# First layer of a two-layer graph network: message weights kept in their own PSUM bank, added rows in PSUM, linear terms at the head of a step

## The chip, the cores and the metric

The kernel runs on one core of a Trainium2 chip. The metric is device microseconds of one execution, taken as the median of several. A core has five engines that run side by side, each with its own list of instructions in program order: PE (TensorE: matmuls and transposes, which write PSUM), DVE (VectorE), ACT (ScalarE), POOL (GpSimd, here used to issue indirect gathers) and SP (SyncE, which issues plain DMAs). They meet through semaphores. PSUM, which PE writes, is handed out in banks; this kernel's pools divide eight of them among its stages' tiles.

## The reference, cut to what matters

There are 6250 nodes with 128 features and 206,250 directed edges, sorted by destination. The first layer is a graph attention with 8 heads of 16 features; the second is an equivariant convolution over the same edges, which the change does not touch.

```python
xl = (x @ W_l + b_l).reshape(-1, H, O)
xr = (x @ W_r + b_r).reshape(-1, H, O)
ee = (edge_attr @ W_e).reshape(-1, H, O)
m = leaky_relu(xl[src] + xr[dst] + ee, 0.2)
logits = einsum('eho,ho->eh', m, att)
lmax = segment_max(logits, dst)
exl = exp(logits - lmax[dst])
denom = segment_sum(exl, dst)
alpha = exl / (denom[dst] + 1e-16)
out = segment_sum(xl[src] * alpha[:, :, None], dst)
# then residual + layer norm, FFN of 512 with gelu, layer norm, outer layer norm, second layer
```

## The kernel before, in words

**Stages.** A prologue and `tables` (up to about 225 us) write two tables of projected nodes to DRAM. `attention` is the first layer's loop over edges (about 225 to 2740 us), with `nodes` (residual, layer norms, FFN of finished nodes) fed into it piece by piece. `convolution` is the second layer (to the end).

**Tiles.** A unit is 768 edges, 6 tiles of 128 edges; there are 269 units, and unit k is taken in by step k. Up to 8 units make a batch, 35 in all; most of them have 8. Each edge has 136 values: 8 heads times 17, of which the first 16 are the features of a head and the 17th (`O`) a linear term, the part of the leaky relu that is linear in its input and that can be had from a matmul.

**One step k**, in the order in which the program issues it; since each engine takes its instructions in this order, it is the order of the work on each engine:

- `load(k+2)` (L366, L400 to L406): six gathers of rows of `xl` by POOL, then SP's DMAs for edge attributes, positions, and rows of `xr`.
- `terms(k+1, 0)` and `terms(k+1, 1)`: the pre-activation z of half a unit each, in a PSUM tile of its own (pool `zp`, 3 banks). Matmuls L420 add the edge term and `xr`. The first half gets the rows of `xl` by a matmul with the identity (L423), and then ACT copies its linear terms to `pr` (L426). The second half gets its rows later, on DVE.
- `sum_up` (L551) between the two halves: matmuls that put the sums of an earlier unit into place, in a tile `nd`.
- for a batch whose last unit was E: `rows` at step E+1 (PE transposes the logits, L462, ACT copies them to `lgt`, L463), `peaks` at E+2 (four scans on DVE, L471 to L477, then PE and ACT for `cr`, L482 to L485), `shifts` and `weights` at E+3. `shifts` ends in `gd` and `sd` (L494 to L499). `weights` makes logits minus peak in a PSUM tile (PE, L506 and L508), takes its exp into SBUF as `ex` (ACT, L511), writes the exp of each unit's eight columns into the 17th column of its `xl` (ACT, eight instructions on L514), and makes the scale `s` (PE L516, ACT L518).
- `sums` (L538): twelve matmuls of the weighted rows with a one-hot matrix, into a tile `ag`; ACT copies them to `sb` (L542, L543), which `sum_up` reads one step later.
- `parts(k)` on DVE: L439 multiplies max(z, 0) of the first half by the attention vector; L436 adds z and the rows of `xl` of the second half into `pr` in SBUF, and L439 does the same there.
- a register load on DVE (L597), `places(k+2)` (L411, one-hot of destinations for a later step), `logits` (L445, a reduction of `pr`), `collect` (L557, adds a unit's sums into the accumulator; this frees `nd`).
- for the units that `when` gives this step: `one_hot` (L372) and `messages` (L528, two multiplications of `xl` by `ex` in place, both operands in SBUF).
- one piece of `nodes`.

**PSUM.** Pool `zp` has 3 banks, `mp` 3, `nodes` 2: eight. All tiles named `m` share the three banks of `mp` in turn: `ag` of the sums, `nd`, the transposes, `c_ps`, the weights' `ex_ps` and `s_ps`. A tile waits until the readers of the last tile in its bank are done.

**The plan.** `when` gives the step of each unit's messages: not before E+4, then one unit a step, and two a step near the end (the last 28 units, `ENDING`). Its sums follow one step later, `sum_up` two, `collect` three. An order written in the program is the order of each engine; no scheduler moves instructions.

Of the kernel before, what the change touches and what calls it, by code (L numbers as in the profile page):

```python
# [8 lines left out]
F32 = mybir.dt.float32  # L9
BF16 = mybir.dt.bfloat16  # L10
I32 = mybir.dt.int32
AF = mybir.ActivationFunctionType
OP = mybir.AluOpType
PSUM = bass.MemoryType.PSUM
DRAM = bass.MemoryType.DRAM

P = 128
# [16 lines left out]
R8 = U * 8  # L34
TU = 6
UE = TU * P
W = 32
H = 8
O = D // H
OW = O + 1  # L40
# [67 lines left out]
class Fast:  # L108
# [269 lines left out]
    def attention(self, acc, xlp, xls):  # L378
# [3 lines left out]
        tc, nc, a, NU = self.tc, self.nc, self.a, self.NU  # L382
        with ExitStack() as st:
            def pool(n, b, **k):
                return st.enter_context(tc.tile_pool(name=n, bufs=b, **k))
            ld, wk, b1, b2 = pool("ld", 3), pool("wk", 2), pool("b1", 1), pool("b2", 2)
            zp, mp = pool("zp", 3, space=PSUM), pool("mp", 3, space=PSUM)
            last = b1.tile([H, 1], F32, name="last0")
            nc.vector.memset(last, -BIG)
            of = {u: (b, u - v) for b, (v, m, _) in enumerate(self.batches) for u in range(v, v + m)}  # L390
            ohs, eas, zs, prs, lgs, ms, sbs, nds = {}, {}, {}, {}, {}, {}, {}, {}
# [21 lines left out]
            def terms(u, half):  # L413
                ea, _, xr = eas[u]
                xl, oht = xls[u], ohs[u]
                z = zs[u, half] = zp.tile([P, 3 * ZW], F32, name="z")
                for lhs, rhs in ((ea, self.w3[:, 2]), (oht, xr)):
                    for t in range(3):
                        e = slice((3 * half + t) * P, (3 * half + t + 1) * P)
                        nc.tensor.matmul(z[:, t * ZW:(t + 1) * ZW], lhs[:, e], rhs,  # L420
                                         start=(t == 0 and lhs is ea), stop=(half == 1 and t == 2 and lhs is oht))
                if half == 0:
                    nc.tensor.matmul(z, self.ident, xl[:, :3, :].rearrange("p t f -> p (t f)"),  # L423
                                     start=False, stop=True)
                    prs[u] = wk.tile([P, TU * H, OW], F32, name="pr")
                    nc.scalar.activation(prs[u][:, :3 * H, O], z.rearrange("p (h o) -> p h o", o=OW)[:, :, O], AF.Copy)  # L426
                else:
                    del eas[u], ohs[u]

            def parts(u):  # L430

                for k in range(2):
                    z = zs.pop((u, k)).rearrange("p (h o) -> p h o", o=OW)
                    p = prs[u][:, 3 * H * k:3 * H * (k + 1)]
                    if k:
                        nc.vector.tensor_add(p.rearrange("p h o -> p (h o)"), z.rearrange("p h o -> p (h o)"),  # L436
                                             xls[u][:, 3:, :].rearrange("p t f -> p (t f)"))
                        z = p
                    nc.vector.scalar_tensor_tensor(p[:, :, :O], z[:, :, :O], 0.0, self.attb, op0=OP.max, op1=OP.mult)  # L439

            def logits(u):
                b, i = of[u]
# [59 lines left out]
            def weights(b):  # L502
                R, gd, sd = ws[b]
                lg = lgs.pop(b)
                ex_ps = mp.tile([P, TU, R], F32, name="m")
                nc.tensor.matmul(ex_ps, self.ident, lg[:, :, :R], start=True, stop=False)  # L506
                for t in range(TU):
                    nc.tensor.matmul(ex_ps[:, t, :], gd[:R, t * P:(t + 1) * P], self.negi[:R, :R],  # L508
                                     start=False, stop=(t == TU - 1))
                ex = b2.tile([P, TU, R8], F32, name="ex")  # L510
                nc.scalar.activation(ex[:, :, :R], ex_ps, AF.Exp)  # L511
                for i in range(R // H):
                    xv = xls[self.batches[b][0] + i].rearrange("p t (h o) -> p t h o", o=OW)
                    nc.scalar.activation(xv[:, :, :, O], ex_ps[:, :, i * H:(i + 1) * H], AF.Exp)  # L514
                s_ps = mp.tile([P, U], F32, name="m")
                nc.tensor.matmul(s_ps, self.e128[:R], sd[:R], start=True, stop=True)  # L516
                s = b2.tile([P, U], F32, name="s", bufs=3)
                nc.scalar.activation(s, s_ps, AF.Copy)  # L518
                ws[b] = ex, s

            def messages(u):

                b, i = of[u]
                xl = xls.pop(u)
                xv = xl.rearrange("p t (h o) -> p t h o", o=OW)[:, :, :, :O]
                for t in range(0, TU, 3):
                    v = xv[:, t:t + 3]
                    nc.vector.tensor_mul(  # L528
                        v, v, ws[b][0][:, t:t + 3, i * H:(i + 1) * H, None].to_broadcast([P, 3, H, O]))
                ms[u] = xl, ohs.pop(u)  # L530

            def sums(u):

                xl, oh = ms.pop(u)
                ag = mp.tile([P, ZW], F32, name="m")
                for t in range(TU):
                    q = t % 4
                    nc.tensor.matmul(ag[q * W:(q + 1) * W], oh[:, t, :], xl[:, t, :],  # L538
                                     start=(t < 4), stop=(t + 4 >= TU))
                sb = sbs[u] = wk.tile([P, 2, D], F32, name="sb")  # L540
                av = ag.rearrange("p (h o) -> p h o", o=OW)
                nc.scalar.activation(sb[:, 0].rearrange("p (h o) -> p h o", o=O), av[:, :, :O], AF.Copy)  # L542
                nc.scalar.activation(sb[:, 1].rearrange("p (h o) -> p h o", o=O),  # L543
                                     av[:, :, O:].to_broadcast([P, H, O]), AF.Copy)

            def sum_up(units):
                nd = mp.tile([P, 2, 2, W], F32, name="m")
                for i, u in enumerate(units):
                    sb = sbs.pop(u)
                    for j in range(2):  # L550
                        nc.tensor.matmul(nd[:, i, j], sb[:, j], self.s4, start=True, stop=True)  # L551
                    nds[u] = nd[:, i]
# [4 lines left out]
                nc.vector.scalar_tensor_tensor(v, v, ws[b][1][:, i:i + 1], nds.pop(u), op0=OP.mult, op1=OP.add)  # L557


            when, ready, k = {}, 0, 0  # L560
            for u in range(NU):
                end = self.batches[of[u][0]][2]
                k = max(k, end + (4 if end < NU - 1 else 3))
                busy = {k - 2, k - 3} & {b[2] for b in self.batches}
                if len(when.get(k, ())) == (2 if k >= NU or k > NU - ENDING and not busy else 1):
                    k += 1
                when.setdefault(k, []).append(u)

            AHEAD = 2
            ends = {end: b for b, (_, _, end) in enumerate(self.batches)}  # L570
# [3 lines left out]
            for half in range(2):  # L574
                terms(0, half)
            for k in range(max(when) + 4):
                now, sums_of, ups_of, got = (when.get(k - i, []) for i in range(4))
                if k + AHEAD < NU:
                    load(k + AHEAD)
                if k == 2:  # L580
                    nodes = Queue(self.nodes(st, acc), self.done, 2)
                if k + 1 < NU:
                    terms(k + 1, 0)
                if ups_of:
                    sum_up(ups_of)
                if k + 1 < NU:
                    terms(k + 1, 1)
                if k - 3 in ends:
                    shifts(ends[k - 3])
                    weights(ends[k - 3])  # L590
                if k - 2 in ends:
                    peaks(ends[k - 2])
                for u in sums_of:
                    sums(u)
                if k < NU:
                    parts(k)
                cs = [nc.vector.value_load(self.r0[0:1, u:u + 1], min_val=0, max_val=self.n) for u in got]  # L597
                if k + AHEAD < NU:
                    places(k + AHEAD)
                if k < NU:  # L600
                    logits(k)
                for u, c in zip(got, cs):
                    collect(u, c)
                for u in now:
                    ohs[u] = self.one_hot(wk, u)
                    messages(u)
                if k - 1 in ends:
                    rows(ends[k - 1])
                for _ in range(1 + (k > NU + 3) if k > 1 else 0):
                    nodes.step(max(got, default=-1))  # L610
# [1026 lines left out]
```

## Time and profile before

| what | value |
| --- | --- |
| median of 6 runs | 5966.35 us (5944.16 to 5976.72) |
| the profiled execution's own time | 5954.48 us |
| its span (first to last instruction) | 5952.6 us, so 1.88 us lie around it |
| mean granted TensorE clock | 0.721 of full speed |
| busy: PE, DVE, ACT, POOL | 3948.0 (66%), 2639.9 (44%), 956.0 (16%), 3212.4 (54%) |
| 2780 to 5950 us (second layer): PE, DVE, ACT, POOL busy | 2116.29, 1070.67, 369.12, 1543.84 of 3170 us |
| gathers of the first layer, L366 into `xl` | 1590, mean 1035 ns |
| gathers of the second layer, L366 into `f` | 1614, mean 943 ns |

How to read it: durations of groups are means of one instruction in ns; "idle before" is the time in which the engine had nothing to run just before the group's instructions, and the name behind the arrow is what ended that wait, inferred from semaphore events. "remote" is a release that the records ascribe to no engine of this core, and "issue" a stretch in which the engine waited for nothing that the profile shows. Ends of matmuls are modelled. In a window of the timeline each row is start, duration, engine, line and operation, with the wait ahead of it in brackets.

### The profile page before, as it was taken

To read this page: it belongs to the slowest core of one execution; us is meant where nothing else is said; L and a number is where in the kernel's file an instruction comes from. 1 tells how busy PE (TensorE), PEld (TensorE's weight loads), DVE (VectorE), ACT (ScalarE), POOL (GpSimd) and SP (SyncE) were. 2 spreads that over 40 slices of the span, in tenths; PEclk is the share of its full clock that TensorE was granted. 3 is DMA by queue.
4 is the path that set the end of the run, shared out by engine and by line. 5 is a ranking of instruction groups with operands and counts; after the bars stand their busy time and mean duration, and the time that the engine had idled before them with its cause. 6 is when DMAs were issued, how large, how long until landed. Compare 5 with 4: busy or idle time off the path is not lost.

```text
span 5952.6 us, 67647 instructions
## 1 busy us (share of the span) xinstructions
PE 3948.0 (66%) x21381; PEld 3123.8 (52%) x21381; DVE 2639.9 (44%) x6828; ACT 956.0 (16%) x2528; POOL 3212.4 (54%) x3236
## 2 busy tenths in 40 slices
PE   3666676766666667666666667666666666666666
PEld 2454555555455555445555555555555555555555
DVE  1565556556555556546333333333333333333333
ACT  1111222222222222113111111111111111111111
POOL 6256666666666666652454444544545445454454
PEclk6677777777777777767677776777777767777777
DMA  4444444444434444331111111111111111111111
GB/s 120 128 120 106 105 109 112 114 111 115 113 102 112 108 114 117 102 94 51 39 42 36 41 41 38 42 37 39 42 38 38 40 40 41 39 41 37 39 42 35
DMA packets 290621, 428.25 MB, mean 72 GB/s; under 512 B 122700, under 2 KB 199454, under 8 KB 290254
## 3 DMA queue, kind: packets, MB, share of 16 engines
q0 software_dynamic: 103296, 218.27, 15.5%
q1 hardware_dynamic: 183258, 197.74, 11.3%
q10 hardware_dynamic: 3700, 7.82, 0.4%
q8 instruction: 173, 2.83, 0.2%
q14 instruction: 194, 1.59, 0.1%
HBM read 403.55 MB, written 19.96 MB: 71 GB/s over the span
## 4 chain that ended last, share of the span: by engine, by line
PE 29%; another core or an unknown queue 23%; ACT 4%; issue 2%; DVE 2%; DVEq 0%; DMA 0%; POOL 0%; ACTq 0%
PE y L850 8%; PE h_ps L803 8%; PE w L810 6%; PE y L848 5%; ACT h L804 2%; PE z L420 1%; PE m L538 0%; DVE xl L528 0%; ACT L623 0%; ACT L804 0%; DVE pr L439 0%; PE z L423 0%; ACT v L632 0%; PE n L702 0%
## 5 line engine op out<-in xcount | busy, mean ns | idle before, releaser
L366 POOL DMA_INDIRECT f<-fFEAT,fsrc x1614 | 1522.6, 943 | 1604.5 <-PE y L850 1135.3
L366 POOL DMA_INDIRECT xl<-fXL,fsrc x1590 | 1645.5, 1035 | 999.4 <-issue 425.8
L822 DVE SCALAR_TENSOR_TENSOR os<-at,fl,e 128x128 f32<-128x128 f32 x1614 | 454.4, 344 | 1819.4 <-remote 1013.7
L803 PE MATMUL h_ps<-e,m 128*128 128x384 f32 (+1 forms) x540 | 407.3, 856 | 858.7 <-ACT h L804 853.8
L850 PE MATMUL y<-os,f 128*128 128x96 f32 x3228 | 892.6, 367 | 0.1
L848 PEld LDWEIGHTS y<-os,f 128*128 128x128 f32 x3228 | 704.3, 254 | 190.9 <-issue 80.9
L420 PE MATMUL z<-fw,ea 128*128 128x136 f32 x3228 | 659.4, 350 | 140.4 <-issue 61.2
L804 ACT ACTIVATE h<-h_ps 128x384 f32<-128x384 f32 x540 | 264.6, 490 | 2742.0 <-remote 1280.3
L803 PEld LDWEIGHTS h_ps<-e,m 128*128 128x128 f32 (+1 forms) x540 | 157.2, 322 | 980.6 <-ACT h L804 951.2
L420 PEld LDWEIGHTS z<-fw,ea 128*128 128x128 f32 x3228 | 558.7, 243 | 212.5 <-issue 111.2
L848 PE MATMUL y<-os,f 128*128 128x32 f32 x3228 | 654.7, 290 | 1.6 <-DVE f L831 1.6
L850 PEld LDWEIGHTS y<-os,f 128*128 128x128 f32 x3228 | 649.5, 249 | 0.2 <-DVE f L831 0.2
L810 PE MATMUL w<-wq,h 128*128 128x256 f32 x1620 | 562.7, 482 | 0.0
L538 PE MATMUL m<-xl,oh 128*32 128x136 f32 x3228 | 260.5, 351 | 261.9 <-ACT s L518 92.7
L831 DVE TENSOR_TENSOR f<-w,f 128x384 f32<-128x384 f32 (+1 forms) x810 | 408.7, 546 | 0.0
L810 PEld LDWEIGHTS w<-wq,h 128*128 128x128 f32 x1620 | 356.8, 244 | 41.0 <-issue 0.6
L551 PEld LDWEIGHTS m<-fcst,sb 128*128 128x128 f32 x1076 | 192.4, 236 | 346.6 <-issue 146.6
L803 PE MATMUL h_ps<-h,m 128*128 128x384 f32 x540 | 248.8, 545 | 169.4 <-ACT h L804 145.6
L551 PE MATMUL m<-fcst,sb 128*128 128x32 f32 x1076 | 182.7, 301 | 207.8 <-ACT sb L543 106.1
L423 PE MATMUL z<-xl,fcst 128*128 128x408 f32 x538 | 312.3, 668 | 8.2 <-issue 8.1
L538 PEld LDWEIGHTS m<-xl,oh 128*32 128x32 f32 x3228 | 131.4, 127 | 323.4 <-issue 117.4
L528 DVE TENSOR_TENSOR xl<-xl,ex 128x384 f32<-128x384 f32 x538 | 274.0, 549 | 8.1 <-ACT ex L511 8.1
(145 smaller groups left out, 4093.5 us busy)
## 6 DMA issues: line engine op xcount, KB each, us to landing
ea<-fast_eat_dram SPq DMA_DIRECT2D x269, 384.0 KB
lb<-fLB SPq DMA_DIRECT2D x269, 144.0 KB
f<-fFEAT,fsrc POOLq DMA_INDIRECT x1614
xl<-fXL,fsrc POOLq DMA_INDIRECT x1590
xr<-fXR SPq DMA_DIRECT2D x807, 8.5 KB
e<-fast_e8t_dram SPq DMA_DIRECT2D x16, 384.0 KB
fXR<-pt SPq DMA_DIRECT2D x16, 306.0 KB
fXL<-tb SPq DMA_DIRECT2D x16, 204.0 KB
```

The source lines that it names most:

```text
L366: self.nc.gpsimd.indirect_dma_start(out=to, out_offset=None, in_=table, in_offset=bass.IndirectOffsetOnAxis(ap=self.src[:, g:g + 1], axis=0))
L420: nc.tensor.matmul(z[:, t * ZW:(t + 1) * ZW], lhs[:, e], rhs, start=(t == 0 and lhs is ea), stop=(half == 1 and t == 2 and lhs is oht))
L423: nc.tensor.matmul(z, self.ident, xl[:, :3, :].rearrange("p t f -> p (t f)"), start=False, stop=True)
L538: nc.tensor.matmul(ag[q * W:(q + 1) * W], oh[:, t, :], xl[:, t, :], start=(t < 4), stop=(t + 4 >= TU))
L551: nc.tensor.matmul(nd[:, i, j], sb[:, j], self.s4, start=True, stop=True)
L803: nc.tensor.matmul(ps, m, x[:, s], start=True, stop=True)
L804: nc.scalar.activation((h1s, hs)[k][p][:, s], ps, AF.Gelu_apprx_tanh, scale=sc)
L810: nc.tensor.matmul(w[:, 2 * t:2 * t + 2, :], hs[p][:, e:e + P], wq, start=True, stop=True)
L822: nc.vector.scalar_tensor_tensor(os[:, 2 * t + i], at4, self.l[:, 2 * p + i, c * CT + t:c * CT + t + 1], e4s[p][:, 2 * (c * CT + t) + i, : ...
L831: nc.vector.tensor_mul(vy[:, :, j, 32:].rearrange("p t (c x) -> p t c x", c=3), w[:, :, None, 64 + j * 32:96 + j * 32].to_broadcast([P, n, ...
L848: nc.tensor.matmul(ys[p][:, i, 0], vy[:, e, 0], os[:, e, 3], start=(c == t == i == 0), stop=False)
L850: nc.tensor.matmul(ys[p][:, i, 1:], vy[:, e, 1], os[:, e, :3], start=False, stop=last)
```

## The change

Three things are edited, all of them in `attention`:

1. **Linear terms and additions at the head of a step.** A new function `linear(k)` is the first of step k. On DVE it adds the rows of `xl` to z of the second half, in PSUM and in place (L435 of the new kernel), and on ACT it copies the linear terms of both halves to `pr` (L436, twice a step). Before, only the first half's were copied, one step earlier, right behind L423, and the second half's came out of the addition. `parts` is left with two multiplications (L443), both from PSUM. The register load moves ahead of `parts`.
2. **Message weights in a PSUM bank of their own.** A new pool `xp` with one bank holds `ex`; `mp` goes from 3 banks to 2. The exp is taken in place in PSUM (L515), the eight columns are copied from it (L518, Copy in place of Exp), and the messages (L532) read their factor from PSUM.
3. **The place of `weights`.** Before, it always stood behind `shifts` in step E+3, ahead of the sums. Now a dictionary `due` says where: ahead of the sums as before for 8 of the 35 batches (the first four and the last four), and for the other 27 at the end of step E+3, behind that step's messages (the last ones of the batch before) and ahead of `rows` and of the piece of `nodes`. The steps that `when` gives to the messages are the same in both kernels.

```diff
@@ -384,7 +384,7 @@
             def pool(n, b, **k):
                 return st.enter_context(tc.tile_pool(name=n, bufs=b, **k))
             ld, wk, b1, b2 = pool("ld", 3), pool("wk", 2), pool("b1", 1), pool("b2", 2)
-            zp, mp = pool("zp", 3, space=PSUM), pool("mp", 3, space=PSUM)
+            zp, mp, xp = pool("zp", 3, space=PSUM), pool("mp", 2, space=PSUM), pool("xp", 1, space=PSUM)
             last = b1.tile([H, 1], F32, name="last0")
             nc.vector.memset(last, -BIG)
             of = {u: (b, u - v) for b, (v, m, _) in enumerate(self.batches) for u in range(v, v + m)}
@@ -422,21 +422,26 @@
                 if half == 0:
                     nc.tensor.matmul(z, self.ident, xl[:, :3, :].rearrange("p t f -> p (t f)"),
                                      start=False, stop=True)
-                    prs[u] = wk.tile([P, TU * H, OW], F32, name="pr")
-                    nc.scalar.activation(prs[u][:, :3 * H, O], z.rearrange("p (h o) -> p h o", o=OW)[:, :, O], AF.Copy)
                 else:
                     del eas[u], ohs[u]
 
+            def linear(u):
+
+
+                prs[u] = wk.tile([P, TU * H, OW], F32, name="pr")
+                for k in range(2):
+                    z = zs[u, k]
+                    if k:
+                        nc.vector.tensor_add(z, z, xls[u][:, 3:, :].rearrange("p t f -> p (t f)"))
+                    nc.scalar.activation(prs[u][:, 3 * H * k:3 * H * (k + 1), O],
+                                         z.rearrange("p (h o) -> p h o", o=OW)[:, :, O], AF.Copy)
+
             def parts(u):
 
                 for k in range(2):
                     z = zs.pop((u, k)).rearrange("p (h o) -> p h o", o=OW)
-                    p = prs[u][:, 3 * H * k:3 * H * (k + 1)]
-                    if k:
-                        nc.vector.tensor_add(p.rearrange("p h o -> p (h o)"), z.rearrange("p h o -> p (h o)"),
-                                             xls[u][:, 3:, :].rearrange("p t f -> p (t f)"))
-                        z = p
-                    nc.vector.scalar_tensor_tensor(p[:, :, :O], z[:, :, :O], 0.0, self.attb, op0=OP.max, op1=OP.mult)
+                    nc.vector.scalar_tensor_tensor(prs[u][:, 3 * H * k:3 * H * (k + 1), :O], z[:, :, :O], 0.0,
+                                                   self.attb, op0=OP.max, op1=OP.mult)
 
             def logits(u):
                 b, i = of[u]
@@ -502,16 +507,15 @@
             def weights(b):
                 R, gd, sd = ws[b]
                 lg = lgs.pop(b)
-                ex_ps = mp.tile([P, TU, R], F32, name="m")
-                nc.tensor.matmul(ex_ps, self.ident, lg[:, :, :R], start=True, stop=False)
+                ex = xp.tile([P, TU, R], F32, name="ex")
+                nc.tensor.matmul(ex, self.ident, lg[:, :, :R], start=True, stop=False)
                 for t in range(TU):
-                    nc.tensor.matmul(ex_ps[:, t, :], gd[:R, t * P:(t + 1) * P], self.negi[:R, :R],
+                    nc.tensor.matmul(ex[:, t, :], gd[:R, t * P:(t + 1) * P], self.negi[:R, :R],
                                      start=False, stop=(t == TU - 1))
-                ex = b2.tile([P, TU, R8], F32, name="ex")
-                nc.scalar.activation(ex[:, :, :R], ex_ps, AF.Exp)
+                nc.scalar.activation(ex, ex, AF.Exp)
                 for i in range(R // H):
                     xv = xls[self.batches[b][0] + i].rearrange("p t (h o) -> p t h o", o=OW)
-                    nc.scalar.activation(xv[:, :, :, O], ex_ps[:, :, i * H:(i + 1) * H], AF.Exp)
+                    nc.scalar.activation(xv[:, :, :, O], ex[:, :, i * H:(i + 1) * H], AF.Copy)
                 s_ps = mp.tile([P, U], F32, name="m")
                 nc.tensor.matmul(s_ps, self.e128[:R], sd[:R], start=True, stop=True)
                 s = b2.tile([P, U], F32, name="s", bufs=3)
@@ -557,10 +561,14 @@
                 nc.vector.scalar_tensor_tensor(v, v, ws[b][1][:, i:i + 1], nds.pop(u), op0=OP.mult, op1=OP.add)
 
 
-            when, ready, k = {}, 0, 0
+
+            when, due, k = {}, {}, 0
             for u in range(NU):
-                end = self.batches[of[u][0]][2]
-                k = max(k, end + (4 if end < NU - 1 else 3))
+                b, i = of[u]
+                end = self.batches[b][2]
+                if i == 0:
+                    due[max(k, end + 3), k < end + 3] = b
+                    k = max(k + 1, end + (4 if end < NU - 1 else 3))
                 busy = {k - 2, k - 3} & {b[2] for b in self.batches}
                 if len(when.get(k, ())) == (2 if k >= NU or k > NU - ENDING and not busy else 1):
                     k += 1
@@ -575,6 +583,8 @@
                 terms(0, half)
             for k in range(max(when) + 4):
                 now, sums_of, ups_of, got = (when.get(k - i, []) for i in range(4))
+                if k < NU:
+                    linear(k)
                 if k + AHEAD < NU:
                     load(k + AHEAD)
                 if k == 2:
@@ -587,14 +597,15 @@
                     terms(k + 1, 1)
                 if k - 3 in ends:
                     shifts(ends[k - 3])
-                    weights(ends[k - 3])
+                if (k, True) in due:
+                    weights(due[k, True])
                 if k - 2 in ends:
                     peaks(ends[k - 2])
                 for u in sums_of:
                     sums(u)
+                cs = [nc.vector.value_load(self.r0[0:1, u:u + 1], min_val=0, max_val=self.n) for u in got]
                 if k < NU:
                     parts(k)
-                cs = [nc.vector.value_load(self.r0[0:1, u:u + 1], min_val=0, max_val=self.n) for u in got]
                 if k + AHEAD < NU:
                     places(k + AHEAD)
                 if k < NU:
@@ -604,6 +615,8 @@
                 for u in now:
                     ohs[u] = self.one_hot(wk, u)
                     messages(u)
+                if (k, False) in due:
+                    weights(due[k, False])
                 if k - 1 in ends:
                     rows(ends[k - 1])
                 for _ in range(1 + (k > NU + 3) if k > 1 else 0):
```

## The prediction

> **What bounds the kernel now.** The change touches only the first layer's loop, from about 225 to 2740 us: 269 steps of one unit (768 edges), 9.3 us each. I read first the windows, then the groups by form, the waits of 300 to 2700 us, and the timeline of single steps.
>
> ```profile
> core 0: us, PE busy (x) PEld busy (x) DVE busy (x) ACT busy (x) POOL busy (x), PEclk, DMA share, GB/s
> 1000.00:1500.00 500.00, 354.00 (x2311) 269.16 (x2310) 302.54 (x688) 112.27 (x362) 335.85 (x320) 0.75 0.43 112
> ```
>
> In 500 us no engine is busy over 354 (PE), DVE 303, ACT 112: nothing is full. The step is a ring of handovers, and the waits say which:
>
> ```profile
> ACT sb L542 <- remote: 414.3, 64, 14.2
> ...
> ACT sb L542 <- PE m L538: 203.0, 106, 6.5
> ...
> DVE pr L439 <- ACT pr L426: 136.2, 47, 10.9
> ...
> PE m L551 <- ACT sb L543: 104.3, 32, 8.6
> ...
> PE m L538 <- ACT s L518: 92.4, 22, 12.3
> ...
> PE z L420 <- DVE pr L439: 40.9, 28, 5.4
> ```
>
> (Waited for: total us, times, longest.) ACT's copies of the sums wait for PE, and PE's next matmul waits for those copies. Part of this is no work at all:
>
> ```profile
> 1056.27 0.66 PE L538 MATMUL m<-xl,oh 128*32 128x136 f32 x12
> ...
> 1062.58 0.94 POOL L366 DMA_INDIRECT xl<-fXL,fsrc  x1 [0.30 <-issue]
> ...
> 1065.51 0.28 ACT L542 ACTIVATE sb<-m 128x128 f32<-128x128 f32 x1 [7.16 <-remote]
> ```
>
> The sums ended at 1056.93; the copy that needs only them began 8.6 us later, while seven gathers ran back to back (1056.34 to 1063.5). I call this the **hold**: over 234 steps the timeline gives a mean of 2.99 us from the end of L538 to the start of L542, about half of them under 0.3.
>
> Step lengths from sums to sums, averaged over the full batches by phase p (steps since the batch's last unit), with the hold in brackets: p0 7.15 (4.78), p1 9.39 (3.34), p2 15.27 (0.73; the scans), p3 12.91 (0.21; shifts and weights), p4 6.39 (3.21), p5 6.32 (3.01), p6 7.18 (6.05), p7 11.41 (2.61). In p3 the sums start 6.59 us after the last term matmul, and the timeline shows why:
>
> ```profile
> 1083.01 0.49 ACT L511 ACTIVATE ex<-m 128x384 f32<-128x384 f32 x1 [3.49 <-remote]
> 1083.39 0.35 ACT L514 ACTIVATE xl<-m 128x48 f32<-128x48 f32 x2
> ...
> 1083.99 1.45 ACT L514 ACTIVATE xl<-m 128x48 f32<-128x48 f32 x6 [0.25 <-DMA xl<-fXL,fsrc]
> ...
> 1085.30 0.17 ACT L518 ACTIVATE s<-m 128x8 f32<-128x8 f32 x1
> 1085.49 0.64 PEld L538 LDWEIGHTS m<-xl,oh 128*32 128x32 f32 x12 [4.17 <-ACT s L518]
> ```
>
> Weights, exp, eight copies and s stand ahead of the sums, which take the bank that they held.
>
> **The change, part by part.** Durations are means of 300 to 2700 us:
>
> ```profile
> L528 DVE TENSOR_TENSOR xl<-xl,ex 128x384 f32<-128x384 f32 x496 | 252.6, 549 | 1.9 <-ACT ex L511 1.9
> L436 DVE TENSOR_TENSOR pr<-z,xl 128x408 f32<-128x408 f32 x250 | 143.6, 574 | 171.8 <-remote 65.6 <-PE z L420 47.6 <-PE z L423 30.0
> L439 DVE SCALAR_TENSOR_TENSOR pr<-pr,fattb 128x384 f32<-128x384 f32 x250 | 140.1, 560 | 8.6
> L439 DVE SCALAR_TENSOR_TENSOR pr<-z,fattb 128x384 f32<-128x384 f32 x251 | 136.9, 545 | 210.9 <-ACT pr L426 136.2 <-issue 74.6
> ```
>
> *Durations: no term.* The addition (0.574) moves ahead of the linear copies and now writes PSUM; no row does that, so I bound it by 0.545 (L439 from PSUM) and 0.99 (the reduction L445, the longest of a step) and take 0.574, the same operation. The second L439 reads PSUM instead of SBUF: 0.545 for 0.560. L528 with one factor in PSUM: between 0.545 and 0.574, now 0.549. The exp in place: 0.49 into SBUF, bounds 0.37 and 0.59 (L463 of both sizes). Eight Exp become eight Copy, 0.253 each, nearest the same. The new second linear copy costs 0.211 of ACT a step (L426); it stands on the path and is in the ring below.
>
> The register load moves from behind the additions and products to ahead of them, on DVE. DVE idles 44.2 us before L411, 0.18 a step, which is the most that it can cost today; ahead of the first L439 it lies beside the wait for ACT's copies: nothing, and 0.18 a step (45 us) if DVE is never early there. No DMA moves: the loads keep their place on SP's and POOL's queues, behind nothing new.
>
> *1. Weights out from ahead of the sums.* 27 of the 35 batches place them at the end of step E+3 (E: the batch's last unit); 8 keep the old place. 27 x 6.59 = **-178 us**.
>
> *2. What is late next.* At the end of E+3 the weights wait for the messages of that step (the one bank of ex), and the linear copies of E+4 are queued behind them on ACT. ACT first does sb(E+3): sums 1.06, hold about 3, copies 0.45, nodes' operations 0.8 (some 200 us in 250 steps, 72 of it table loads of 1.283): 5.3 us after the sums began. Then exp 0.49, eight copies 1.77, s 0.17, linear copies 0.3, and the DVE chain from the first L439 to collect (3.2 now, less the addition and some: 2.5): 10.5, and with PE's weights (0.86 + 1.55 + 0.34) partly ahead of the exp up to 12.8. Before p4 took 6.39: +4.1 to +6.4, I take 5.9: 27 x 5.9 = **+159**. Peaks in p2 now wait for collect and two more copies: 0.8 x 31 = **+25**. Cover that would bring both to nothing: PE's terms of the next unit (3 to 4 us in the timeline), which it can do while ACT is held up; in the ring below they lie beside it already.
>
> *3. The ring of ordinary steps.* With two banks in place of three, the sums of a step wait for that step's collect; collect follows the linear copies, which now stand on ACT behind the last step's sb and nodes' work instead of ahead of it. Ring: sums 1.0, hold H, sb 0.45, nodes 0.8, linear copies 0.3, DVE 2.5, handovers 0.25: 5.3 + H. Against the phases above with H as it is: p0 +2.9, p1 0, p5 +2.0, p6 +4.1, p7 0: 9.0 a batch. Yet holds shrink in longer steps (0.73 and 0.21 in p2 and p3); at half of H: +0.5, +0.5, +1.1 = 2.2. I take 4.8, a little nearer to 2.2: 31 x 4.8 = **+149** (bounds 0 and +280). For no cost speaks that collect ends 2.5 us ahead of the sums on average today, and after their start in only 36 of 220 steps.
>
> *4. Ending.* In the last 28 steps, two units a step, 14 sums wait for a sb copy in place of a free bank: 14 x 2.2 = **+30** (0 to +60).
>
> *5. Less disturbance.* Gathers take 1035 ns here and 943 in the second layer; of 319 gathers over 1.05 us, 104 lie beside an L528 and 72 beside an L439. L528 and the second L439 lose an SBUF operand. POOL itself waits for buffers (314 us behind L543), so only bursts and holds shorten: 7% of 3.0 us in 250 steps, 53 us; and PE gives 10.9 signals a step in place of 12.0 (counted in the two instruction lists), 8% of the holds in some 170 ordinary steps, 40 us: **-93** (bounds -150 and 0).
>
> The Trainium skill (SBUF — State Buffer, Who interferes with whom) says that a VectorE instruction with two SBUF inputs contends with GpSimd instructions that read SBUF, and one with at most one doesn't. The 1035 against 943 ns agree with it; by the rule alone 92 ns x 1590 = 146 us of GpSimd time would go, which I don't put on the path.
>
> **Sum:** -178 + 159 + 25 + 149 + 30 - 93 = +92. The profiled execution took 5954.5 us (span 5952.6 and 1.9 around it), 12 under the median: 5954.5 + 92 = 6046, **6045 us**.
>
> **Rivals.** *Faster:* the weights' new place is hidden: PE's terms and DVE's addition cover the chain in E+4. For: PE waits 92 us for s in 22 places, and after the change none of the sums does. Against: the linear copies are behind it on an in-order engine. With term 2's 159 gone: 92 - 159 = -67, **5887**. It decides if E+4 gives back less than 5.9 - 92/27 = 2.5 us. *No change:* holds take up the slack, term 3 is 2.2 a batch: 92 - 81 = +11, **5965**. *Much slower:* holds stay as they are, term 3 is 9.0: 92 + 130 = +222, **6176**.
>
> **The numbers.** Forecast (5975 to 6140, its own range) 0.42; faster 0.34; no change 0.11; much slower 0.13. A measurement tells about 0.3% (18 us) from no change. So faster 0.34, same 0.11, slower 0.55. The range 5850 to 6180 leaves out the ends of both outer cases, about 0.18.
>
> **What would show it.** Right: the sums (now L542) wait for collect (L561) and no longer for s; the linear copies (L436) run right behind the sb copies (L547) or node work; the first L443 waiting on L436 for more than 136 us in all; p3 down by 6 and p4 up by 4 to 6; gathers near 990 ns. Wrong: p4 about 6.4 (then faster), ordinary steps unchanged with holds shorter (no change), or an L435 or L532 much over 0.6 us, which would add their excess to every step, as DVE is in the ring.

## The result: 0.5% slower, and the profile after

The changed kernel takes 5995.67 us (median of 21 runs, 5974.85 to 6006.81) where the kernel before takes 5966.14 (42 runs): a ratio of 1.0045, 95% interval 1.0036 to 1.0054. The forecast was slower, 6045 us; the sign held, the size did not: +29.5 us in place of +79. (The sum itself was +92, set on the profiled execution, which was 12 us under the median.) Kernels that are compared ran on the same chip, but the experiments fell on several chips; on chip 13 both kernels take over a quarter less time and the change is a gain of 3.1%. That turned out to be the key to the first result.

The profiled execution of the changed kernel has a span of 5981.3 us (before 5952.6). Step lengths, from sums to sums, averaged over the full batches as in the prediction (worked out from the trace's rows):

| phase | p0 | p1 | p2 | p3 | p4 | p5 | p6 | p7 | batch |
| --- | --- | --- | --- | --- | --- | --- | --- | --- | --- |
| before | 7.15 | 9.39 | 15.27 | 12.91 | 6.39 | 6.32 | 7.18 | 11.41 | 76.0 |
| after | 9.79 | 9.36 | 14.63 | 6.39 | 12.22 | 6.45 | 8.69 | 8.58 | 76.1 |

The parts move by up to 6.5 us, and the batch stays. From step 24 to 236 the two traces differ by 2.5 us in 2000. Behind step 236 the changed kernel loses 28 us: 14.7 up to step 267, 13.1 from there to the second layer. Only the 13.1 is safe: the three other traces with three `mp` banks (the kernel before again, and twice with late weights) show 96 to 98 us for that drain, like the first (96.5), and all with two banks on this kind of chip 104 to 112. In the stretch up to 267 two traces of the kernel before itself, from different chips, differ by 23.6 us.

The waits of the changed kernel, 300 to 2700 us (total us, times, longest):

```profile
ACT sb L546 <- remote: 685.3, 81, 14.7
DVE pr L443 <- ACT pr L436: 447.2, 133, 13.3
...
ACT sb L546 <- PE m L542: 248.6, 84, 11.4
...
PE z L420 <- DVE pr L443: 75.5, 58, 5.6
...
PEld m L542 <- DVE acc L561: 30.0, 47, 4.7
```

Nothing waits for s ahead of the sums any more (92.4 us before). In its place DVE waits 447 us for the linear copies (136 before), the sums wait in 47 places for collect, and the copies of the sums wait longer for a release that the records ascribe to no engine (685 us for 414). The durations were costed rightly; by form (out and in, partitions by elements), in the same stretch:

```profile
L443 DVE SCALAR_TENSOR_TENSOR pr<-z,fattb 128x384 f32<-128x384 f32 x498 | 253.5, 550 | 587.9 <-ACT pr L436 447.2 <-issue 54.6 <-ACT h L645 23.7
L532 DVE TENSOR_TENSOR xl<-xl,ex 128x384 f32<-128x384 f32 x497 | 250.3, 543 | 0.0
L435 DVE TENSOR_TENSOR z<-z,xl 128x408 f32<-128x408 f32 x249 | 146.2, 587 | 240.1 <-remote 134.3 <-PE z L420 35.9 <-PE m L542 14.7
L515 ACT ACTIVATE ex<-ex 128x384 f32<-128x384 f32 x30 | 14.7, 488 | 44.1 <-PE z L423 12.8 <-remote 10.9 <-PE ex L513 10.2
```

The addition into PSUM takes 587 ns against 574 into SBUF, the multiplication of the messages 543 against 549, exp in place 488 against 490. The gathers, from the page, became faster as the prediction said (972 ns, before 1035):

```profile
L366 POOL DMA_INDIRECT xl<-fXL,fsrc x1590 | 1545.2, 972 | 1111.0 <-issue 414.1
```

### The profile page after: what moved, and what is told of

The parts are those of the page before. It is cut to its first block, busy times and chain, and to the rows that moved or that the text cites. A ratio compares the mean times of both kernels' runs of the same rounds, so it can differ in the third digit from the quotient of the medians.

```text
span 5981.3 us, 67651 instructions
## 1 busy us (share of the span) xinstructions
PE 4007.9 (67%) x21381; PEld 3168.0 (53%) x21381; DVE 2604.8 (44%) x6828; ACT 969.4 (16%) x2797; POOL 3116.1 (52%) x3236
## 4 chain that ended last, share of the span: by engine, by line
PE 30%; another core or an unknown queue 25%; ACT 4%; issue 2%; DVE 2%; DMA 0%; DVEq 0%; ACTq 0%; POOL 0%
PE y L863 8%; PE h_ps L816 8%; PE w L823 6%; PE y L861 5%; ACT h L817 2%; PE z L420 1%; PE m L542 1%; DVE xl L532 0%; ACT L636 0%; PE z L423 0%; DVE pr L443 0%; PE n L715 0%; PE n L723 0%; PE n L746 0%
## 5 line engine op out<-in xcount | busy, mean ns | idle before, releaser
L366 POOL DMA_INDIRECT xl<-fXL,fsrc x1590 | 1545.2, 972 | 1111.0 <-issue 414.1
L420 PE MATMUL z<-fw,ea 128*128 128x136 f32 x3228 | 681.8, 360 | 209.0 <-issue 110.4
L420 PEld LDWEIGHTS z<-fw,ea 128*128 128x128 f32 x3228 | 576.9, 252 | 283.1 <-issue 187.0
L443 DVE SCALAR_TENSOR_TENSOR pr<-z,fattb 128x384 f32<-128x384 f32 x538 | 273.7, 550 | 605.2 <-ACT pr L436 463.9
L542 PE MATMUL m<-xl,oh 128*32 128x136 f32 x3228 | 245.1, 357 | 202.0 <-ACT sb L547 82.9
L423 PE MATMUL z<-xl,fcst 128*128 128x408 f32 x538 | 316.9, 678 | 2.4 <-issue 2.3
L546 ACT ACTIVATE sb<-m 128x128 f32<-128x128 f32 x269 | 74.6, 277 | 1500.4 <-remote 685.3
```

The costliest lines, as they stand in the source:

```text
L366: self.nc.gpsimd.indirect_dma_start(out=to, out_offset=None, in_=table, in_offset=bass.IndirectOffsetOnAxis(ap=self.src[:, g:g + 1], axis=0))
```

## What paces the middle: the hold, seen in both traces

Why does a batch stay at 76 us? The hold of the prediction has a cause that the first trace already shows, in a stage that I had not read. Up to 225 us POOL issues the first units' gathers while PE, ACT and DVE make the second table. Windows of the kernel before (columns as in the prediction):

```profile
125.00:150.00 25.00, 3.38 (x8) 1.90 (x8) 0.58 (x1) 0.51 (x1) 18.90 (x21) 0.50 0.33 89
150.00:175.00 25.00, 3.38 (x8) 1.90 (x8) 1.07 (x2) 0.94 (x2) 15.62 (x17) 0.50 0.30 62
175.00:200.00 25.00, 16.30 (x39) 9.38 (x40) 13.26 (x22) 8.10 (x17) 0.00 (x0) 0.50 0.47 132
```

With 21 gathers in 25 us PE starts 8 matmuls; with none, 39. Its clock is 0.50 in all three rows. The changed kernel on chip 13, in the same stage, with as many gathers:

```profile
75.00:100.00 25.00, 25.00 (x60) 13.99 (x60) 13.12 (x23) 8.38 (x17) 19.21 (x20) 0.50 0.81 193
```

So on the first kind of chip PE and the engines that wait for it hardly get on while gathers run back to back, and on chip 13 they do. I read this as PE's signals (its semaphore updates) being held. That it is the signal and not the matmul that is late is argued, since ends of matmuls are modelled; the starts speak for it. In the changed kernel's trace the twelve matmuls of a unit's sums start within 0.58 us where gathers run and 0.65 us where none do. And of 126 holds over 2 us between steps 24 and 236, PE has started later matmuls more than 1 us before the copy in 109.

Counted from the trace's semaphore events, in the middle of the loop: before, PE gives 0.71 signals in a gather of usual length, 1.33 in a lengthened one, 0.19 in the 0.3 us pause between two, and 5.7 in a longer gap of POOL (2.7 us); on chip 13, 1.36 in a gather and 0.48 in the pause. (The trace of the kernel before holds 5757 of the 6704 updates that PE's instructions should make, that of the changed kernel on chip 13 holds 6302 of 6444, so the counts are only rough.) A hold in the changed kernel's timeline, with the sums and PE's next work:

```profile
1098.70 0.66 PE L542 MATMUL m<-xl,oh 128*32 128x136 f32 x12
...
1100.08 0.94 POOL L366 DMA_INDIRECT xl<-fXL,fsrc  x1 [0.30 <-issue]
...
1100.27 0.90 PE L423 MATMUL z<-xl,fcst 128*128 128x408 f32 x2
...
1102.58 0.95 POOL L366 DMA_INDIRECT xl<-fXL,fsrc  x1 [0.30 <-issue]
...
1104.91 0.28 ACT L546 ACTIVATE sb<-m 128x128 f32<-128x128 f32 x1 [8.58 <-remote]
1105.08 0.27 ACT L547 ACTIVATE sb<-m 128x128 f32<-128x128 f32 x1
...
1105.62 0.95 POOL L366 DMA_INDIRECT xl<-fXL,fsrc  x1 [2.09 <-ACT sb L547]
```

The burst of gathers ends; PE's signal arrives; the sums are copied; that frees an `xl` buffer; the next burst starts. In the changed kernel a burst of six begins within 0.7 us of a sb copy in 82% of the steps, lasts 7.41 us, and 2.11 us pass to the next: 9.52. Before: 7.80 and 1.75, 9.55. The step is a burst and a gap; my reading, which the experiments test, is that what is reordered inside it is paid for, or won back, from the holds.

## The experiments

**The places and the banks, on chip 3.** Four kernels; the kernel before took 6033.9 us there. The times expected below were worked out for the first chip, where it takes 5966, so I compare by the ratio. The changed kernel itself was not run on chip 3. *The kernel before with only the weights moved:*

```diff
-                    weights(ends[k - 3])
+                if (k, True) in due:
+                    weights(due[k, True])
...
+                if (k, False) in due:
+                    weights(due[k, False])
                 if k - 1 in ends:
                     rows(ends[k - 1])
```

> The kernel before, with nothing but the place of the weights changed: for the same 27 batches they stand at the end of step E+3, behind its messages. Theory (the 6.5 us that step p3 loses to the weights are given back in p4 only because the changed kernel queues its linear copies behind them on ACT; before's linear copies of a step are made one step earlier, so they stay ahead): p3 falls from 12.9 to about 6.5 us, p4 stays at 6.4 to 7.5, so 27 x 5.5 = 150 us less: 5800 to 5870 us. Rival (the chain has to be waited for anyway, by the messages of E+4 or by PE through the banks): p4 rises by 5 to 6 us, and the time stays at 5950 to 5985 us.

6029.11 us, ratio 1.0001 (0.9982 to 1.0019): the rival. p3 fell to 6.47 us, and p4 rose to 14.49, with the linear copies not behind the weights at all. PE shows the new wait (300 to 2700 us):

```profile
PE m L551 <- ACT s L518: 62.6, 14, 9.7
```

sum_up of step E+4 stands ahead of the next terms and sums on PE, and waits for s. *The changed kernel with the linear copies ahead of the weights and nodes:*

```diff
-                if k < NU:
-                    linear(k)
...
+                if k + 1 < NU:
+                    linear(k + 1)
                 if (k, False) in due:
                     weights(due[k, False])
```

> The changed kernel, with the additions and linear copies of unit k+1 moved from the head of step k+1 to the end of step k: behind the messages, but ahead of the weights, of rows and of the piece of nodes. Theory (p4 is long because these copies stand behind exp, eight copies and s): p4 falls from 12.2 to 7 or 8 us, 27 x 4.5 = 120 us, and the other steps lose up to 0.8 us of nodes' ACT work each: 5790 to 5880 us. Rival (p4 is long because the messages and sums of E+4 need ex and s themselves, or because of holds): p4 stays above 11 us, and the time at 5975 to 6005 us.

6042.22 us, 1.0011 (1.0000 to 1.0023), p4 12.09 us: the rival for p4; the ratio makes 5973 us of the first chip, just under its times. My reason for a long p4 fell with both. *The changed kernel with the messages' factor in SBUF:*

```diff
-                nc.scalar.activation(ex, ex, AF.Exp)
+                ex_ps, ex = ex, b2.tile([P, TU, R8], F32, name="exs")
+                nc.scalar.activation(ex[:, :, :R], ex_ps, AF.Exp)
```

> The changed kernel, but exp goes to an SBUF tile as before, the eight columns are exp from PSUM as before, and the messages read their factor from SBUF: two SBUF operands again. Theory (gathers are slowed by DVE instructions with two SBUF operands, and longer bursts mean longer holds): mean gather in the first layer up from 972 to 1000 to 1020 ns, and the time up by 15 to 50 us on the changed kernel: 6010 to 6045 us. Rival (POOL runs ahead and its time isn't on the path): gathers slower in the same way, time within 12 us of the changed kernel's, 5984 to 6008 us.

6025.87 us, 0.9990 (0.9975 to 1.0005). The gathers went to 1066 ns, over the theory's 1000 to 1020, so the messages' second SBUF operand is what slows them; the time did not follow. On the first chip's scale it is 5960 us, under the ranges of both. *The changed kernel with one tile for a step's sums:*

```diff
-                ag = mp.tile([P, ZW], F32, name="m")
+                ag = mp.tile([P, 2, ZW], F32, name="m")
```

> The changed kernel, with the sums of a step's units in one PSUM tile (two units share a bank) and one pair of ACT copies for both; nothing changes in steps with one unit. Theory (the whole loss lies in the ending, where 14 sums wait for the first unit's copies because the second unit's tile needs their bank): the stretch from step 236 to the second layer loses its 28 us again, 5962 to 5975 us. Rival (the ending is longer because the linear copies stand behind four sb copies, or because of holds): at most 10 us less, 5985 to 5997 us.

6029.05 us, 1.0000 (0.9987 to 1.0012). By the ratio alone this is the theory's 5966 us. But the two kernels before it have no joint tile and are level too, and the drain behind step 267 took 106.5 us, in place of 109.6 in the first trace: 3 us, not 28. Four kernels with quite different steps (p4 from 11.9 to 14.5 us) lie within 17 us of each other, and a batch takes 76 to 77 us in all of them. That called for a common cause.

**The suspected cause, halved and increased.** The next runs fell on chip 13, where the kernel before takes 4368.61 us. The kernels with fewer or more gathers, or without the edge term, were run once on a chip.

> The changed kernel once more, for comparison with the kernel before and with the other runs on one chip. Theory (the first comparison holds on every chip): 1.0045 times the kernel before, and a batch of eight steps in the middle as long as before's, 76 us. Rival (four variants were level with the kernel before on another chip, so the difference belongs to the chips): 1.000 to 1.002.

4230.35 us, 0.9684 (0.9663 to 0.9705): neither. The holds were gone: 0.09 us a step, against 2.64, and the copies wait for the sums themselves (waits of 150 to 1750 us, trace of the next run of this kernel):

```profile
ACT sb L546 <- PE m L542: 792.5, 208, 9.2
```

*Three of six gathers replaced by a plain DMA:*

```diff
-                    for t in range(TU):
+                    for t in range(TU // 2):
                         self.gather(xls[u][:, t, :], self.XL, u, t)
+                    nc.sync.dma_start(xls[u][:, TU // 2:, :],
+                                      self.XL[:TU // 2 * P].rearrange("(t p) f -> p t f", p=P))
```

> The changed kernel with three of the six gathers of a unit replaced by one plain DMA of other rows of the same table (the rows of half of the edges are thus left out). Theory A (the length of a batch stays at 76 us whatever is reordered because PE's signals get through slowly while gathers run, and the gathers fill 7.4 of 9.5 us): with 3.7 us of gathers a step, the step falls by 2 us or more, 269 x 2 = 540 us, to 5450 us or less. Theory B (the batch is set by a ring of handovers of PE, ACT and DVE that the reorderings only shift): less than 60 us of change. Theory C (DMA traffic): no gain either, or a loss, since as many bytes move.

4011.14 us, 219 less than the changed kernel beside it, and a batch of 52.9 us in place of 60.5. That lies between theory A's 540 and the 60 of B and C. *A seventh gather:*

```diff
+                    self.gather(b2.tile([P, ZW], F32, name="xtra"), self.XL, u, 0)
```

> The changed kernel with a seventh gather per unit, into a tile that nobody reads. Theory A (gathers set the pace): each step longer by most of the 1.25 us from gather to gather, 200 to 330 us in all. Theory B (ring of PE, ACT and DVE; POOL waits 2.1 us a step for buffers): less than 40 us.

4597.02 us, 367 more, over theory A's 200 to 330: 1.36 us for each of 269 units, a little more than the 1.25 from gather to gather. *No matmuls of the edge term:*

```diff
-                for lhs, rhs in ((ea, self.w3[:, 2]), (oht, xr)):
+                for lhs, rhs in ((oht, xr),):
```

> The changed kernel without the six matmuls of the edge term in each unit (edge attributes are left out of the pre-activations; they are still loaded). PE loses 12 of about 37 records a step, some 3.3 us. Theory D (PE at its granted clock sets the pace, its records' ends being only modelled): a step shorter by 2 to 3.3 us, 540 to 880 us in all. Theory A (gathers): less than 100 us. Theory B (ring, in which the terms of the next unit are one link): 100 to 400 us.

4234.26 us, 4 more than the changed kernel: PE's work is not what paces chip 13. Three of these were repeated on the same chip, and the joint sums were run:

> The changed kernel again, beside the next three on one chip. If the copies of the sums start within 0.3 us of the last sum (no holds, as in the run of 4230 us): 0.965 to 0.972 times the kernel before. If there are holds of 2 to 3 us a step: 1.0035 to 1.0055 times, and 76 us a batch of eight steps.

4231.12 us, 0.9687 (0.9665 to 0.9710).

> The changed kernel with the sums of a step's two units in one PSUM tile, beside the changed kernel itself. Theory (the loss sits in the last 30 steps, where a second tile waits for the first's copies): 15 to 28 us under the changed kernel in this call with holds; without holds 5 to 20 us under it. Rival (the ending's length has another cause): within 8 us of it.

4229.17 us, 0.9694 (0.9672 to 0.9716): 2 us under the changed kernel, no difference that can be told.

> The changed kernel with three of six gathers replaced by a plain DMA (the rows of half of the edges are left out). Where PE's signals are held: theory A (they get through at 0.6 to 0.85 a us while a gather runs and 2.4 otherwise) says that with 3.7 us of gathers a step, a step falls from 9.5 by 1.5 to 3 us, 400 to 800 us in all. Theory B (the ring's links, whatever POOL does): under 60 us. Theory E (holds come with DMA traffic, which is as large as before): under 60 us, and holds as long as in the changed kernel. Without holds: 4000 to 4020 us as the first time.

> The changed kernel with a seventh gather per unit that nobody reads. Where PE's signals are held: theory A, 1.25 us more of slow signals a step, 0.9 to 1.3 us a step or 240 to 350 us in all. Theory B (POOL waits 2.1 us a step for buffers, so that a seventh fits): under 60 us. Without holds: 4580 to 4610 us as the first time.

4012.69 and 4587.93 us, as before. Here the gathers set the pace outright. Changed kernel on chip 13, the page's group, then waits of 150 to 1750 us:

```profile
L366 POOL DMA_INDIRECT xl<-fXL,fsrc x1590 | 1559.8, 981 | 490.9 <-issue 395.6
```

```profile
POOL xl L366 <- issue: 302.3, 992, 0.3
PE z L423 <- DMA xl<-fXL,fsrc: 183.5, 94, 4.6
```

POOL is busy or in its 0.3 us pause and waits for no buffer in those rows; PE waits for rows to land. 48 gathers of 0.981 + 0.30 us make 61.5 us, and a batch takes 60.4.

**Parts of the change, on chip 15** (holds again; the kernel before 6039.07 us).

> The kernel before itself, for its trace. Without holds (a time of about 4365 us) I expect the sums of p3 to wait for the weights by 5 to 7 us as in the first trace, gathers of about 1040 ns, and a batch of some 65 us against 60.4 of the changed kernel; POOL without a wait for buffers in most steps if gathers set the pace (theory A'), with waits of 1 us or more a step if the weights do (theory W).

6037.58 us, a batch of 77.3 us, gathers of 1029 ns, p3 14.01. So its trace without holds was not to be had.

> The kernel before with only the weights moved to the end of step E+3. Without holds: theory W (the weights ahead of the sums are what costs) expects 0.968 to 0.98 times the kernel before; theory A' (gathers pace the middle, and they stay slow) expects 0.99 to 1.005. With holds: 0.998 to 1.002 as on the other chip.

6035.14 us, 1.0000 (0.9986 to 1.0015), as on chip 3. *The changed kernel with additions and linear copies as before (L426, L436 and L439 of the kernel before), everything else changed:*

```diff
-                if k < NU:
-                    linear(k)
...
+                    if k:
+                        nc.vector.tensor_add(p.rearrange("p h o -> p (h o)"), z.rearrange("p h o -> p (h o)"),
+                                             xls[u][:, 3:, :].rearrange("p t f -> p (t f)"))
+                        z = p
```

> The changed kernel with the additions and linear copies as they were before (an addition into SBUF in parts, one linear copy behind the first half's terms); weights late, and ex in its own bank. Without holds: theory W expects it to keep most of the gain, or more of it, as the linear copies no longer stand behind the weights: 0.955 to 0.972 of the kernel before. Theory A' expects part of it only, since one DVE operation has two SBUF operands again: 0.972 to 0.99. With holds: 0.998 to 1.006.

6019.72 us, 0.9967 (0.9955 to 0.9978), just under the expected 0.998 to 1.006: a gain of 0.3% where there are holds, from the weights' place and bank without the head of the step. The place alone gave none beside it (1.0000).

> The changed kernel with ex in SBUF for the messages. Without holds: theory A' (gathers set the pace; on the other chip this put them up from 970 to 1066 ns) expects 6 x 0.09 us more a step, 269 x 0.55 = 150 us: 1.0 to 1.006 of the kernel before, so the whole gain gone. Theory W expects a loss under 40 us: 0.968 to 0.978. With holds: 0.998 to 1.002 as on the other chip.

6029.78 us, 0.9986 (0.9971 to 1.0000), gathers 1060 ns. What it was for, a run without holds, did not come.

**The decisive run, on chip 3 with holds.** The half of the gathers once more:

> The changed kernel with three of six gathers replaced by a plain DMA (the rows of half of the edges are left out). With holds: theory A (PE gives 0.5 to 0.7 signals per gather and 2.4 a us in the pauses, in the traces with holds) expects 3.7 us less of gathers a step, and 1.5 to 3 us less a step: 76 us a batch falls to 52 to 64, 5200 to 5600 us in all. Theory B (the ring of PE, ACT and DVE sets the pace): at least 74 us a batch. Theory D (PE's real pace, whatever POOL does): at least 74 us a batch. Without holds: 53 us a batch, 4010 us, as twice before.

5251.94 us, 784 less than the kernel before beside it (6036.39). A batch falls from 76 to 54.1 us, and the hold from 2.64 to 0.27 us a step. Its windows in the table stage and in the middle, its group and its first wait (300 to 2000 us):

```profile
100.00:125.00 25.00, 7.24 (x17) 4.31 (x18) 3.05 (x7) 1.94 (x5) 11.65 (x13) 0.50 0.21 52
125.00:150.00 25.00, 25.00 (x61) 14.04 (x60) 19.53 (x32) 9.54 (x19) 0.00 (x0) 0.50 0.68 200
```

```profile
1000.00:1500.00 500.00, 410.95 (x3129) 327.41 (x3128) 397.58 (x926) 150.21 (x557) 212.67 (x219) 0.87 0.57 156
```

```profile
L366 POOL DMA_INDIRECT xl<-fXL,fsrc x795 | 774.6, 974 | 1123.3 <-ACT sb L549 532.7
```

```profile
ACT sb L548 <- PE m L544: 707.6, 230, 7.0
```

As soon as the table stage's gathers end, PE goes from 7.24 to 25.00 us busy in 25. In the middle no wait for a "remote" release is left at the head of the list; the sums' copies wait for the sums themselves. As many bytes move, DMA is busier (0.57 for 0.43), and yet the step is shorter: it is the gathers, not the traffic. (POOL's instruction and its indirect transfer went together; this run does not separate them.) PE does the same matmuls as in the changed kernel: it is not PE's own pace. *The last kernel joins the two edits that had looked useful:*

> The changed kernel with additions and linear copies as in the kernel before, and the sums of two units in one PSUM tile. Theory (weights late and ex in PSUM are worth having, the linear copies behind sb are what costs): with holds 0.993 to 0.998 of the kernel before; without holds 0.955 to 0.97, as good as the changed kernel (0.9687) or better. Rival (the head of the step is what brings the gain where there are no holds, since both DVE operations read PSUM): without holds 0.975 to 0.995.

6014.26 us, 0.9962 (0.9947 to 0.9976), level with the kernel without the joint tile. With holds, it and that one are below the kernel before, where the changed kernel (1.0045) is above it. But the three come from different sets of runs, and the 1.0045 from the first alone; on chip 13 neither of the two was run.

## Why the prediction was right in sign and wrong in size

- **Durations: no term.** Right, as the rows of after show.
- **Term 1, weights ahead of the sums (-178).** Right where it stands: p3 fell by 6.52 us a batch, costed at 6.59.
- **Term 2, what is late next (+159, +25).** p4 rose by 5.83 us, costed at 5.9, but for another reason. The text had the linear copies behind the weights on ACT; with these out of the way p4 stays at 12.1 us, and without them it is 14.5. With the weights moved alone, sum_up waits for s in 14 places (62.6 us); in the changed kernel only in 7 (23.6 us). Which of s, the sums' copies, ex and the holds ends p4 last is not settled. p2 fell by 0.64 in place of rising by 0.8, which makes 20 us less in place of 25 more.
- **Term 3, the ring (+149), the step that failed.** "Ring: ... 5.3 + H" treats the hold as a delay that is added to other links. The ordinary phases p0, p1, p5, p6 and p7 rose by 1.42 us a batch together, 44 us in 31 batches, where the ring alone gave 4.8. Term 5 took 3.0 off, so that the two together (1.8) look right; but term 5 is worth nothing here, as shown below, and the two errors hid each other. In all the batch was to rise by 1.9 us and rose by 0.08; 1.4 of this miss is p2. With measured sizes the sum is -176 + 157 - 20 + 44 + 0, about nothing, and the ending. What the runs show in place of the ring is a step of a burst of gathers and a gap. The parts move by up to 8 us and the batch stays at 76 to 77 us. With half of the gathers it falls to 54.1, and the mean hold from 2.64 to 0.27 us. So a hold is no fixed link. That it ends when the burst lets PE's signals through, and is shorter the later the sum, is my reading of this. The rival "no change: holds take up the slack" (5965 us) named this mechanism at 0.11; it had the middle right.
- **Term 4, the ending (+30).** The 14 sums that wait for sb are there. In 2400 to 2850 us, before and after:

```profile
PE m L538 <- ACT sb L543: 37.8, 8, 12.5
```

```profile
PE m L542 <- ACT sb L547: 82.9, 14, 12.1
```

  The kernel's plan has 19 steps with two units, from step 242 on; the prediction counted 14. In the two first traces the middle is level and the difference lies behind step 236. Of that, 13 us go with two banks in all kernels; the other 15 are less than two traces of one kernel differ there, so where they lie stays open. One tile for both units, which takes that wait away, gave back 3 to 9 us of the drain, and on chip 13 nothing that the times can tell; what makes the rest of the 13 us is not shown.
- **Term 5, less disturbance (-93).** The gathers fell to 972 ns (about 990 forecast), 100 us of POOL's time. With holds it is worth nothing: the burst shrinks by 0.39 us and the gap behind it grows by 0.36, and the two kernels that undo it (1060 and 1066 ns) are not slower than the kernel before, 0.9986 and 0.9990. The rule of the Trainium skill (SBUF — State Buffer, Who interferes with whom) that a VectorE instruction with two SBUF inputs contends with GpSimd's reads agrees with the runs for the messages: 1060 to 1066 ns with such messages, 966 to 976 without. But the kernels of 973 and 976 ns keep one product a step with both operands in SBUF (L439 of the kernel before), so that one costs the gathers little or nothing.
- **Faster, 5887 (0.34).** Its sign came true on chip 13, with 0.9687 where 5887 us means 0.987, but hardly by its mechanism. Where POOL never waits, 48 gathers of 1035 ns and 0.30 us make 64.1 us a batch against 61.5 at 981: 2.6 us for 33.6 batches, 87 us of the 133 measured. This is an estimate, with the 1035 ns taken from a chip with holds; no trace of the kernel before without holds was taken, and no part of the change was run there alone, so which part brings the 3.1% stays open.

## What to carry to other kernels

When a trace shows an engine waiting long after the work it waits for has ended, find what else runs in just these stretches, in every stage of the kernel, before any wait is costed: a delay that belongs to another engine's burst, as here, is not added to a chain but can absorb what is moved in it. If several reorderings leave the period of a loop alone, halve one engine's work at a time: here two such kernels, with half of the gathers and without the edge term, told what sets the pace. And a change can have one sign on a chip where such a burst holds up the others and the other sign on a chip where it does not, so measure on both.

## What the runs showed of the hardware

- Chips differ: the kernel before takes 5966 to 6039 us (medians) in the first measurement and on chips 3 and 15, and 4364 to 4369 on chip 13. Instructions of POOL and DVE last as long there (gathers 981 against 972 ns, L532 542 against 543); what differs is that PE's signals pass during gathers, 1.36 a gather against 0.5 to 0.7. The mean granted TensorE clock differs too (0.85 to 0.87 against 0.72), but not in the table stage, where it is 0.50 in the rows above on both kinds and PE starts 60 matmuls beside 20 gathers in place of 8 beside 21. On chip 3 it rose in the middle to 0.87 with half of the gathers (0.74 in the changed kernel's first trace).
- The second layer, whose code is the same in both kernels, shows the same: 3134 to 3166 us with holds in all these runs, 2037 to 2038 on chip 13, at 943 to 946 ns a gather in both.
- More signals arrive in a longer gather of the kernel before (1.33 in those over 1 us, 0.71 in the others), and making gathers faster did not shorten a step on a chip with holds.
- Why chips differ in this was not to be seen in the traces.
